# Two narrow key tiles of a diagonal in one attention step, and the transposes of a block ahead of both copies

## The chip, the cores and the metric

The kernel runs on one core of a Trainium2 chip, in 32-bit floats throughout. The metric is the device time of one launch in microseconds (us), the median of several runs; lower is better. The core has five engines that work beside each other and wait for each other through semaphores: TensorE (PE in the profile, PEld for its weight loads), VectorE (DVE), ScalarE (ACT), GpSimd (POOL) and SyncE (SP), which here issues most of the DMAs. Each takes its own instructions in order.

## The reference, as far as it matters

The input x is 4096 tokens (32 nodes by 128 time steps) of 256 features. Layer 0 is a pre-normed attention over all 4096 tokens with 8 heads of 32, and a residual; a query of time t sees all keys of time up to t, at every node:

```
x  = (h - mu) / sqrt(var + eps) * ln_g + ln_b
q  = x @ wq.T + bq + sym_emb            # then Q, K, V through in_w; K and V from h, not normed
scores = einsum('bqhd,bkhd->bhqk', Q, K) / sqrt(32)
t = tile(arange(128), 32);  scores = where(t[None, :] > t[:, None], -inf, scores)
ctx = softmax(scores) @ V
h  = h + alpha * (ctx @ out_w.T + out_b)
```

Layer 1 is a banded attention of width 24 and a mixture of 8 experts with two hidden layers each. The change does not touch layer 1.

## The kernel before

**Tiling.** The tokens are sorted by time, so that the mask is block-triangular: 8 blocks of 512 queries (`BLK`, `NBLK`), keys in tiles of 128 (4 time steps by 32 nodes, `P`). Block b attends to key tiles 0 to 4b+3. The first 4b+1 of them are of use to all 512 queries; the last three of the four on the diagonal are of use to the last 384, 256 and 128 queries alone. These three are the narrow tiles. The 8 heads lie in two groups of 4 (`NGRP`, `HG`), a group's 4 heads of 32 features on the 128 partitions.

**A step** is one key tile of one group of one block: 8 x 2 x 4(b+1), 288 steps in all. In it

- `scores` (L1273) makes 4 matmuls, one head each, on 4 row tiles of the array: head 0 into the bank `sa` (pool `ps_a`, one buffer), heads 1 to 3 into three banks `sb` (pool `ps_b`, two buffers). Every matmul of 32-bit floats shows as two passes in the trace;
- `exps` (L1288) makes two exponentials on ScalarE, one of `sa`, one of `sb`, into an SBUF tile `pt` (pool `pp`, 5 buffers); on a diagonal tile POOL then zeroes what the mask forbids inside the 128 x 128 corner, in three memsets (L1298);
- `add` (L1301) adds `pt` to the running sum `acc` on DVE, two heads to an instruction (L1314), which gives the softmax's denominators;
- `product` (L1318) makes 4 matmuls with the values, one head each, on 4 column tiles, into the one bank `av` that stays open for a group's whole pass.

**The order of the work.** It is written out by hand in the loop at L1451 (`manual_schedule`: each engine takes its instructions in the order of the program). Iteration n issues scores of step n, the product of step n-2 (`LAG`), the exponentials of n with a group's last copy of `av` (`evacuate`, L1338) between the two, the add of step n-1, and then what else is due. `key_order` (L1251) spreads the three narrow tiles evenly among the full ones, so each is a step of its own.

**What else is due.** `todo` is the preparation of the next block in pieces (`prep`, L1033): the transposition of its inputs (`transposed_x`, L979: for each of two halves of the features four transposes into a bank, then a ScalarE copy), two projections for keys, two for values, two for queries. They are spread evenly over the steps of the block (L1499), each takes a `ps_b` buffer. Two iterations after a group's last scores its last product is made; one later `close_sums` (L1345) sums `acc` over the partitions with a matrix of ones; in blocks 6 and 7 the last one and two tiles (`direct`, L1267) are not added on DVE but summed there by TensorE too. Six iterations after the last product comes `invert` (reciprocal, and two DMAs on SP that spread it, L1391 and L1394), twelve after it `scale` (DVE, L1402). `stat_at` (L1433) gives the iterations at which DVE takes the layer norm's statistics of blocks 2 to 7, two tiles an iteration from n = 0 to 11; when the last is taken, `rstd_block` (L952) has ScalarE take a square root, for which it changes its function table and back. `load_at` (L1437) gives the iterations at which SP issues the loads for them. In the last group of block 7 POOL adds a bias to 12 tiles of tokens (L1523, L904), from its fifth step on.

Of the kernel before, what the change touches and what calls it, by code (L numbers as in the profile page):

```python
# [10 lines left out]
F32 = mybir.dt.float32  # L11
# [5 lines left out]
P = 128  # L17
# [806 lines left out]
def fast_kernel(ctx: ExitStack, tc: tile.TileContext, ins: dict, out: bass.AP, narrow):  # L824
# [101 lines left out]
    with ExitStack() as l0:  # L926
# [52 lines left out]
        def transposed_x(b, pss):  # L979
            xg = xblk[b]  # L980
            hT = px.tile([P, 2, BLK], F32, tag="hT", name=f"hT{b}", bufs=1)
            for c in range(2):
                for i in range(TPB):
                    nc.tensor.transpose(
                        pss[c][:, i * P : (i + 1) * P], xg[:, i, c * P : (c + 1) * P], ident
                    )
                nc.scalar.copy(hT[:, c, :], pss[c])
            return hT
# [249 lines left out]
        with ExitStack() as at:  # L1238
# [12 lines left out]
            def key_order(b):  # L1251

                n = TPB * (b + 1)
                order, part = list(range(n - TPB + 1)), list(range(n - 1, n - TPB, -1))
                if b == 0:
                    return list(range(n))
                for i, j in enumerate(part):
                    order.insert((i + 1) * n // TPB, j)
                return order

            orders = [key_order(b) for b in range(NBLK)]
            steps = [
                (b, g, j)
                for b in range(NBLK) for g in range(NGRP) for j in orders[b]
            ]

            direct = [orders[b][TPB * (b + 1) - max(0, b - NBLK + 3) :] for b in range(NBLK)]  # L1267

            LAG = 2
            first_col = lambda b, j: max(0, j - TPB * b) * P  # L1270
            raw, held, live, open_av = {}, {}, {}, {}

            def scores(b, g, j):  # L1273
                q = qblk[b]
                lo = first_col(b, j)
                sa = ps_a.tile([P, BLK], F32, tag="a", name=f"sa{b}_{g}_{j}")
                sb = ps_b.tile([P, HG - 1, BLK], F32, tag="b", name=f"sb{b}_{g}_{j}")
                for h in range(HG):
                    rows = slice(h * HD, (h + 1) * HD)
                    nc.tensor.matmul(  # L1280
                        (sb[:, h - 1, :] if h else sa)[:, lo:],
                        lhsT=kT[rows, g, j * P : (j + 1) * P],
                        rhs=q[rows, g, lo:],
                        start=True, stop=True,
                    )
                raw[b, g, j] = sa, sb

            def exps(b, g, j, between):  # L1288
                lo = first_col(b, j)
                pt = pp.tile([P, HG, BLK], F32, tag="pt", name=f"pt{b}_{g}_{j}")  # L1290
                sa, sb = raw.pop((b, g, j))
                nc.scalar.activation(pt[:, 0, lo:], sa[:, lo:], AF.Exp, scale=SCALE)  # L1292
                between()
                nc.scalar.activation(pt[:, 1:, lo:], sb[:, :, lo:], AF.Exp, scale=SCALE)  # L1294
                if j >= TPB * b:

                    for k in range(1, TT):
                        nc.gpsimd.memset(pt[k * N : (k + 1) * N, :, lo : lo + k * N], 0.0)  # L1298
                held[b, g, j] = pt

            def add(b, g, j):  # L1301

                if j == orders[b][0] or j in direct[b]:
                    return
                pt, lo = held[b, g, j], first_col(b, j)
                if j == orders[b][1]:
                    old = held[b, g, orders[b][0]]
                    live[b, g] = ap.tile([P, HG, BLK], F32, tag="acc", name=f"acc{b}_{g}")
                    if lo:
                        nc.vector.tensor_copy(live[b, g][:, :, :lo], old[:, :, :lo])  # L1310
                else:
                    old = live[b, g]
                for hs in (slice(0, HG // 2), slice(HG // 2, HG)):
                    nc.vector.tensor_tensor(  # L1314
                        live[b, g][:, hs, lo:], old[:, hs, lo:], pt[:, hs, lo:], op=ALU.add
                    )

            def product(b, g, j):  # L1318
                if j == orders[b][0]:
                    open_av[b, g] = ps_av.tile([P, BLK], F32, tag="av", name=f"av{b}_{g}")  # L1320
                av = open_av[b, g]
                pt, lo = held[b, g, j], first_col(b, j)
                for h in range(HG):
                    nc.tensor.matmul(  # L1324
                        av[h * HD : (h + 1) * HD, lo:],
                        lhsT=v[:, j, (g * HG + h) * HD : (g * HG + h + 1) * HD],
                        rhs=pt[:, h, lo:],
                        start=(j == orders[b][0]), stop=(j == orders[b][-1]),
                    )
# [15 lines left out]
            def close_sums(b, g):  # L1345

                sums = banks(f"sums{b}_{g}", 1)[0]
                parts = [held.pop((b, g, j)) for j in direct[b]] + [live.pop((b, g))]
                for k, part in enumerate(parts):
                    for h in range(HG):  # L1350
                        nc.tensor.matmul(  # L1351
                            sums[h * HD : (h + 1) * HD, :], lhsT=ones, rhs=part[:, h, :],
                            start=(k == 0), stop=(k == len(parts) - 1),
                        )
# [69 lines left out]
            def begin_projections():  # L1424
# [8 lines left out]
            stat_at = {  # L1433
                2 * (b - 2) + k: [(b, 2 * k), (b, 2 * k + 1)]
                for b in range(2, NBLK) for k in range(2)
            }
            load_at = {3: ("xs", 5, 6), 4: ("xs", 7), 6: ("xg", 2), 8: ("xg", 3)}  # L1437
# [13 lines left out]
            for n in range(len(steps) + LAG + 1 + 16):  # L1451
                if n < len(steps):
                    b, g, j = steps[n]
                    own = NGRP * TPB * (b + 1)
                    k = orders[b].index(j)
# [16 lines left out]
                    scores(b, g, j)  # L1472
                ends = None
                if 0 <= n - LAG < len(steps):
                    if n - LAG == len(steps) - 1:
                        begin_projections()
                    product(*steps[n - LAG])
                    bb, gg, jj = steps[n - LAG]
                    if jj == orders[bb][-1]:
                        ends = bb, gg  # L1480
                        later.setdefault(n + 1, []).append((close_sums, ends))
                        if ends != LASTU:
                            later.setdefault(n + 6, []).append((invert, ends))
                            later.setdefault(n + 12, []).append((scale, ends))

                def between():
                    if ends:
                        evacuate(*ends)

                if n < len(steps):  # L1490
                    exps(b, g, j, between)
                else:
                    between()
                if 0 <= n - 1 < len(steps):
                    add(*steps[n - 1])
                if n < len(steps):
                    at_step = g * TPB * (b + 1) + k + 1
# [992 lines left out]
```

## Time and profile before

| what | value |
|---|---|
| median of 3 runs | 1527.48 us (1526.95 to 1528.06) |
| the profiled execution, its own time | 1528.81 us |
| its span | 1526.8 us |
| mean granted TensorE clock | 0.997 |
| layer 0's steps, first scores to the last add | 19.1 to 733.3 us |
| from there to the end | 793.5 us |
| ScalarE, an exponential of 128x512 / 128x1536 | 598 / 1451 ns |
| DVE, an add of 128x1024 | 1217 ns |

By block of layer 0, from its first scores to the next block's (us, of the profiled execution):

| block | from | length | PE busy | DVE busy | ScalarE busy |
|---|---|---|---|---|---|
| 0 | 19.11 | 32.67 | 31.76 | 17.21 | 17.22 |
| 1 | 51.78 | 46.72 | 43.35 | 33.96 | 34.88 |
| 2 | 98.50 | 69.17 | 65.14 | 53.62 | 47.14 |
| 3 | 167.67 | 79.63 | 77.95 | 65.86 | 62.13 |
| 4 | 247.30 | 99.00 | 96.52 | 87.35 | 78.79 |
| 5 | 346.30 | 113.31 | 111.20 | 103.77 | 93.36 |
| 6 | 459.61 | 130.04 | 127.94 | 119.04 | 108.89 |
| 7, to the last add | 589.65 | 143.62 | 139.78 | 136.64 | 123.02 |

Reading it: busy time counts an engine's instructions without overlap; a matmul's end is modelled, so a PE that is busy all the time need not run at its peak. What an engine waited for stands in brackets behind an instruction of the timeline: the idle time ahead of it, and the instruction that ended it. "pt L1294" is the exponential of three heads, "pt L1292" that of the first.

### The profile page before, as it was taken

To read this page: it belongs to the slowest core of one execution; us is meant where nothing else is said; L and a number is where in the kernel's file an instruction comes from. 1 tells how busy PE (TensorE), PEld (TensorE's weight loads), DVE (VectorE), ACT (ScalarE), POOL (GpSimd) and SP (SyncE) were. 2 spreads that over 40 slices of the span, in tenths; PEclk is the share of its full clock that TensorE was granted. 3 is DMA by queue.
4 is the path that set the end of the run, shared out by engine and by line. 5 is a ranking of instruction groups with operands and counts; after the bars stand their busy time and mean duration, and the time that the engine had idled before them with its cause. 6 is when DMAs were issued, how large, how long until landed. Compare 5 with 4: busy or idle time off the path is not lost.

```text
span 1526.8 us, 23826 instructions
## 1 busy us (share of the span) xinstructions
PE 1477.1 (97%) x8873; PEld 836.9 (55%) x8873; DVE 1200.6 (79%) x2193; ACT 940.8 (62%) x1402; POOL 163.9 (11%) x387
## 2 busy tenths in 40 slices
PE   8999999999999999999999999999999999999998
PEld 5333232232222222222557887888888788788887
DVE  5667879898899898999746777777786777677775
ACT  4667777877888888988445444544355454544443
POOL 2110003000000000031062002100010000000000
PEclk9999999999999999999999999999999999999999
DMA  6111101010000010000332343333433334343442
GB/s 140 35 43 26 29 8 31 9 29 8 1 15 9 1 49 15 8 9 1 116 116 92 102 132 109 121 104 112 129 121 120 106 104 138 103 128 111 138 152 64
DMA packets 96378, 110.16 MB, mean 72 GB/s; under 512 B 17949, under 2 KB 85232, under 8 KB 96256
## 3 DMA queue, kind: packets, MB, share of 16 engines
q1 hardware_dynamic: 93280, 106.87, 23.5%
q8 instruction: 72, 1.18, 0.3%
q0 software_dynamic: 1888, 0.91, 0.3%
q10 hardware_dynamic: 1088, 0.79, 0.2%
q14 instruction: 50, 0.41, 0.1%
HBM read 98.87 MB, written 8.53 MB: 70 GB/s over the span
## 4 chain that ended last, share of the span: by engine, by line
PE 75%; DVE 12%; ACT 7%; issue 4%; DMA 0%; POOL 0%; ACTq 0%; DVEq 0%; POOLq 0%
PE psh L1948 18%; PE sa L1280 15%; PE av L1324 14%; PE psy L2005 11%; DVE acc L1314 2%; ACT h L1931 2%; PE psv L1026 2%; PE psq L1005 2%; PE psk L992 2%; ACT pt L1294 2%; PE psk L1697 2%; PE sb L1280 1%; PE sums L1351 1%; DVE h L1990 1%; ACT pt L1292 1%
## 5 line engine op out<-in xcount | busy, mean ns | idle before, releaser
L1314 DVE TENSOR_TENSOR acc<-acc,pt 128x1024 f32<-128x1024 f32 (+3 forms) x500 | 529.3, 1127 | 40.7 <-ACT pt L1294 28.4
L1294 ACT ACTIVATE pt<-sb 128x1536 f32<-128x1536 f32 (+3 forms) x288 | 387.6, 1346 | 3.2 <-PE sb L1280 3.0
L1280 PE MATMUL sa<-q,kT 32*128 32x512 f32 (+3 forms) x576 | 303.1, 606 | 9.4 <-ACT pt L1292 7.1
L1280 PE MATMUL sb<-q,kT 32*128 32x512 f32 (+3 forms) x1728 | 307.0, 606 | 1.8 <-ACT pt L1294 0.7
L1931 ACT ACTIVATE h<-h,bshift,bscale 128x256 f32<-128x256 f32 x244 | 159.1, 699 | 221.5 <-DVE h L1990 221.5
L1324 PE MATMUL av<-pt,v 128*32 128x512 f32 (+3 forms) x2304 | 287.1, 571 | 1.5 <-ACT big_t L1339 0.4
L2005 PE MATMUL psy<-wo,h 128*128 128x256 f32 x1024 | 242.8, 380 | 0.0
L1292 ACT ACTIVATE pt<-sa 128x512 f32<-128x512 f32 (+3 forms) x288 | 162.2, 563 | 95.6 <-PE sb L1280 63.9
L2005 PEld LDWEIGHTS psy<-wo,h 128*128 128x128 f32 x1024 | 192.0, 190 | 28.9 <-issue 2.9
L1280 PEld LDWEIGHTS sa<-q,kT 32*128 32x128 f32 x576 | 84.5, 183 | 220.6 <-ACT pt L1292 179.4
L1324 PEld LDWEIGHTS av<-pt,v 128*32 128x32 f32 x2304 | 45.6, 108 | 200.4 <-issue 183.2
L2013 DVE SCALAR_TENSOR_TENSOR tokens<-psy,w,tokens 128x256 f32<-128x256 f32 x256 | 111.0, 475 | 34.9 <-PE psy L2005 34.6
L1975 DVE TENSOR_TENSOR u<-psh,u 128x256 f32<-128x256 f32 x122 | 51.0, 418 | 104.1 <-ACT u L1974 103.8
L1298 POOL MEMSET pt<- 32x128 f32 (+2 forms) x192 | 58.5, 304 | 627.0 <-ACT pt L1294 523.5
L1931 ACT ACTIVATE h<-psh,bshift,bscale 128x256 f32<-128x256 f32 (+1 forms) x132 | 75.6, 574 | 45.8 <-PE psh L1948 38.7
L1280 PEld LDWEIGHTS sb<-q,kT 32*128 32x128 f32 x1728 | 88.3, 183 | 9.1 <-ACT pt L1294 5.8
L1974 ACT COPY u<-psh 128x256 f32<-128x256 f32 x122 | 43.9, 360 | 79.6 <-PE psh L1948 79.2
L1948 PE MATMUL psh<-tx,s 128*128 128x256 f32 x366 | 90.3, 383 | 0.3 <-DVE tx L1921 0.3
L1948 PE MATMUL psh<-th,s 128*128 128x256 f32 x366 | 89.0, 379 | 0.0
L1990 DVE TENSOR_TENSOR h<-psh,u 128x512 f32<-128x512 f32 x122 | 83.1, 681 | 4.2 <-PE psh L1948 4.2
L1948 PEld LDWEIGHTS psh<-tx,s 128*128 128x128 f32 x366 | 70.1, 192 | 10.3 <-DVE tx L1921 0.7
L1948 PE MATMUL psh<-xfT,w 128*128 128x256 f32 x244 | 74.0, 385 | 1.1 <-DVE u L1975 1.1
(332 smaller groups left out, 1764.5 us busy)
## 6 DMA issues: line engine op xcount, KB each, us to landing
w<-in_L_ffn_W_dram SPq DMA_DIRECT2D x128, 256.0 KB
s<-kept SPq DMA_DIRECT2D x56, 512.0 KB
wo<-in_L_ffn_Wo_dram SPq DMA_DIRECT2D x64, 256.0 KB
xg<-in_x_dram SPq DMA_DIRECT2D x32, 128.0 KB
tokens<-in_x_dram SPq DMA_DIRECT2D x8, 512.0 KB
kept<-s SPq DMA_DIRECT2D x8, 512.0 KB
out_dram<-tokens SPq DMA_DIRECT2D x32, 128.0 KB
rec<-flat SPq DMA_DIRECT2D x60, 64.0 KB
```

The lines of the kernel that those rows point to most:

```text
L1280: nc.tensor.matmul((sb[:, h - 1, :] if h else sa)[:, lo:], lhsT=kT[rows, g, j * P : (j + 1) * P], rhs=q[rows, g, lo:], start=True, stop=True,)
L1292: nc.scalar.activation(pt[:, 0, lo:], sa[:, lo:], AF.Exp, scale=SCALE)
L1294: nc.scalar.activation(pt[:, 1:, lo:], sb[:, :, lo:], AF.Exp, scale=SCALE)
L1298: nc.gpsimd.memset(pt[k * N : (k + 1) * N, :, lo : lo + k * N], 0.0)
L1314: nc.vector.tensor_tensor(live[b, g][:, hs, lo:], old[:, hs, lo:], pt[:, hs, lo:], op=ALU.add)
L1324: nc.tensor.matmul(av[h * HD : (h + 1) * HD, lo:], lhsT=v[:, j, (g * HG + h) * HD : (g * HG + h + 1) * HD], rhs=pt[:, h, lo:], start=(j == ...
L1931: nc.scalar.activation(dst, src, AF.Relu, bias=bshift[:, m, k : k + 1], scale=bscale[:, m, k : k + 1])
L1948: nc.tensor.matmul(ps, lhsT=w, rhs=x, start=start, stop=True, skip_group_check=True)
L1975: nc.vector.tensor_tensor(u, a[:, 1], u, op=ALU.add)
L1990: nc.vector.tensor_tensor(flat.rearrange("p (k c) -> p k c", k=2), self.q, self.u.unsqueeze(1).to_broadcast([P, 2, HB]), op=ALU.add,)
L2005: nc.tensor.matmul(ps[:, i, :], lhsT=ht[:, c, r * P : (r + 1) * P], rhs=wo[k][:, c, :], start=(c == 0), stop=(c == 1),)
L2013: nc.vector.scalar_tensor_tensor(out=tokens(n), in0=ps[:, i, :], scalar=w[:, r, e : e + 1], in1=tokens(n), op0=ALU.mult, op1=ALU.add,)
```

## The change

1. `transposed_x` makes all eight transposes of a block first and then the two copies; before, the second four stood behind the first copy.
2. A group's pass is now a list of steps of parts (`unit_steps`). A part is (group, key tile, first query, place in the bank, width). The tiles of 384 and of 128 queries make one step (`both`): the 128 go to columns 0 to 127, the 384 to columns 128 to 511 of the same banks. From block 1 on, group 0's last step holds its own tile of 256 queries and the same tile of group 1 side by side; group 1 uses it from there (`carried`): its product comes with that of group 1's first step, its add with group 1's first add. In block 0 the 256 stay a step of their own.
3. So there are 265 steps instead of 288: 6 in block 0, 8b+5 in block b. A merged step has 8 matmuls of scores, two exponentials, three memsets and one `pt`. The preparation's pieces are spread over the fewer steps.
4. The adds: 384 in two instructions, 128 in one of four heads; the carried 256 in two, and group 1's first pair of tiles then in four of 256 columns. `direct` keeps one tile of each group in block 6 and two in block 7; of group 0 in block 7 these are the last full tile and its half of the shared step, in block 6 the last full tile.
5. The statistics take ten iterations, three tiles in each of the first four, and the loads for them move up by one iteration.

```diff
@@ transposed_x
                         pss[c][:, i * P : (i + 1) * P], xg[:, i, c * P : (c + 1) * P], ident
                     )
+            for c in range(2):
                 nc.scalar.copy(hT[:, c, :], pss[c])
@@ the steps
-            orders = [key_order(b) for b in range(NBLK)]
-            direct = [orders[b][TPB * (b + 1) - max(0, b - NBLK + 3) :] for b in range(NBLK)]
+            def unit_steps(b, g):
+                n = TPB * b
+                order = [[(g, j, 0, 0, BLK)] for j in range(n + 1)]
+                both = [(g, n + 1, P, P, BLK - P), (g, n + 3, BLK - P, 0, P)]
+                order.insert((n + 2) // 2, both)
+                if not b:
+                    order.append([(g, n + 2, BLK // 2, 0, BLK // 2)])
+                elif not g:
+                    order.append(
+                        [(k, n + 2, BLK // 2, k * BLK // 2, BLK // 2) for k in range(NGRP)]
+                    )
+                return order
+            for b, count in ((NBLK - 2, 1), (NBLK - 1, 2)):
+                last = len(units[b, 0]) - 1
+                direct[b, 0] = tuple(range(last - 1, last - 1 + count))
+                last = len(units[b, 1]) - 1
+                direct[b, 1] = tuple(range(last + 1 - count, last + 1))
@@ scores
-                for h in range(HG):
-                    nc.tensor.matmul(
-                        (sb[:, h - 1, :] if h else sa)[:, lo:],
-                        lhsT=kT[rows, g, j * P : (j + 1) * P],
-                        rhs=q[rows, g, lo:],
+                for gg, j, lo, at, w in units[b, g][k]:
+                    for h in range(HG):
+                        nc.tensor.matmul(
+                            (sb[:, h - 1, :] if h else sa)[:, at : at + w],
+                            lhsT=kT[rows, gg, j * P : (j + 1) * P],
+                            rhs=q[rows, gg, lo : lo + w],
@@ add
+                if k == 0 and more:
+                    for hs in HEADS:
+                        nc.vector.tensor_tensor(
+                            live[b, g][:, hs, lo:], pt[:, hs, lo:], other[:, hs, at : at + w],
+                            op=ALU.add,
+                        )
...
+                    if more:
+                        z = more[1][2]
+                        for hs in HEADS:
+                            nc.vector.tensor_tensor(
+                                live[b, g][:, hs, :z], first[:, hs, :z], pt[:, hs, :z],
+                                op=ALU.add,
+                            )
+                            nc.vector.tensor_tensor(
+                                live[b, g][:, hs, z:], live[b, g][:, hs, z:], pt[:, hs, z:],
+                                op=ALU.add,
+                            )
+                        return
...
+                for _, _, lo, at, w in parts:
+                    for hs in HEADS if w > P else (slice(0, HG),):
@@ product
+                todo = [(held[b, g, k], p) for p in units[b, g][k] if p[0] == g]
+                if not k and carried(b, g):
+                    todo.append(carried(b, g))
+                for i, (pt, (_, j, lo, at, w)) in enumerate(todo):
+                    for h in range(HG):
+                        nc.tensor.matmul(
+                            av[h * HD : (h + 1) * HD, lo : lo + w],
@@ statistics and loads
-            stat_at = {
-                2 * (b - 2) + k: [(b, 2 * k), (b, 2 * k + 1)]
-                for b in range(2, NBLK) for k in range(2)
-            }
-            load_at = {3: ("xs", 5, 6), 4: ("xs", 7), 6: ("xg", 2), 8: ("xg", 3)}
+            for n in range(10):
+                count = 3 if n < 4 else 2
+                stat_at[n], tiles_left = tiles_left[:count], tiles_left[count:]
+            load_at = {2: ("xs", 5, 6), 3: ("xs", 7), 5: ("xg", 2), 7: ("xg", 3)}
@@ the loop
-                    own = NGRP * TPB * (b + 1)
+                    own = sum(len(units[b, i]) for i in range(NGRP))
```

## The prediction

> **What bounds the kernel now.** I read the page first, then the stretches of layer 0 block by block, then the timeline of a narrow tile, of a transposition and of a change of head group.
>
> ```profile
> PE 1477.1 (97%) x8873; PEld 836.9 (55%) x8873; DVE 1200.6 (79%) x2193; ACT 940.8 (62%) x1402; POOL 163.9 (11%) x387
> ...
> PE 75%; DVE 12%; ACT 7%; issue 4%; DMA 0%; POOL 0%; ACTq 0%; DVEq 0%; POOLq 0%
> ```
>
> TensorE holds three quarters of the chain, but a share over the whole span hides stages. Of the stretches (start:end, its length, then busy time of PE, PEld, DVE, ACT, POOL), these are block 6 and the last 64 us of layer 0:
>
> ```profile
> 459.61:589.65 130.04, 127.94 (x961) 33.97 (x961) 119.04 (x114) 108.89 (x122) 7.35 (x25) 1.00 0.06 18
> ...
> 669.49:733.27 63.78, 60.96 (x488) 15.48 (x484) 63.77 (x56) 53.48 (x58) 15.44 (x23) 1.00 0.03 9
> ```
>
> In block 6 PE is full and DVE has 11 us to spare; in the last head group of block 7 DVE is full. So an edit pays in blocks 0 to 6 what it takes from PE, and in block 7 what it takes from DVE's adds. A narrow tile on PE, in block 6 (start, length, instruction):
>
> ```profile
> 541.48 1.06 PE L1324 MATMUL av<-pt,v 128*32 128x512 f32 x8
> 542.48 0.37 PE L1280 MATMUL sa<-q,kT 32*128 32x128 f32 x1
> ...
> 542.69 0.27 PE L1280 MATMUL sa<-q,kT 32*128 32x128 f32 x1
> ...
> 542.91 1.07 PE L1324 MATMUL av<-pt,v 128*32 128x512 f32 x8
> ...
> 545.97 0.69 PE L1280 MATMUL sa<-q,kT 32*128 32x512 f32 x1
> ...
> 547.04 0.43 PE L1324 MATMUL av<-pt,v 128*32 128x128 f32 x8
> 547.78 0.69 PE L1280 MATMUL sa<-q,kT 32*128 32x512 f32 x1 [0.31 <-ACT pt L1292]
> ```
>
> Each matmul is two passes. Scores of 512 columns take 1.07 us (545.97 to 547.04), a product of 512 1.00, together the 2.07 us a full step takes. Scores of 128 take 0.43 (542.48 to 542.91), and their product 0.74 (547.04 to 547.78): 0.31 of it is PE waiting until ScalarE has read the one sa bank. A small product cannot cover that exponential.
>
> **The transposes** (all of one block's eight before either copy). Today PE stops between the halves:
>
> ```profile
> 108.19 0.65 PE L984 MATMUL pst<-ident,xg 128*128 128x128 f32 x4
> 108.88 0.59 ACT L987 COPY hT<-pst 128x512 f32<-128x512 f32 x1 [1.07 <-PE pst L984]
> ...
> 109.52 0.66 PE L984 MATMUL pst<-ident,xg 128*128 128x128 f32 x4 [0.68 <-ACT hT L987]
> ```
>
> The second four need nothing of that copy but its place in the order. Seven blocks (1 to 7) are transposed inside the step loop; PE's gaps there are 0.68 us six times and 0.95 once (at 61.45): 5.0 us. The copies then lie back to back on ScalarE while PE runs the next scores, 1.07 us, and ScalarE had waited 1.07 us for the first. I take the whole 5.0; the least, if exponentials are then late, is 2.
>
> **384 with 128.** By the same reading at 573.66 and 578.69, a 384 tile costs 0.89 for scores and 0.78 for its product, 1.67; the 128 costs 0.43 + 0.74 = 1.17. Removed: 2.84. Added is one step of 512 columns, but in twice the matmuls. The mean score pass in the groups by shape is 642, 533, 426 and 321 ns for 512, 384, 256 and 128 columns, so 107 ns per 128; passes start 0.53 and 0.21 apart for 512 and 128, so about 0.1 of each pass is paid whatever its width. The merged scores have four passes, 1.07 + 0.21 = 1.28, which agrees with 0.89 + 0.43 = 1.32; I take 1.30. Products fall 607, 498, 391, 285, the same slope; 1.00 less 2 x 0.43 leaves 0.14 per set, so merged products take 1.14. Step: 2.44; gain 0.40. It is now long enough that nobody waits for the sa bank. The bounds: 2.07, if the second set's fixed part hides (gain 0.77), and no gain.
>
> [...] The second set goes to the same four row groups. A weight load takes 183 ns in the scores and 108 in the products (rows of PEld); exposed for each of the two added passes this is 0.37 + 0.22 = 0.59 on top, 3.03 for the pair, a loss of 0.19. But the row at 542.69 is a second pass to the same row groups, 0.21 after the first and not 0.107 + 0.183 = 0.29. I go by the row.
>
> **256 with the other group's 256.** Today both cost 0.65 (492.14 to 492.79) + 0.74 (498.83 to 499.57) = 1.39, 2.78 a block. The shared step stands last in group 0; its scores take 1.30 beside a full product of 1.00. Its own product falls on the change of group, where ScalarE waits for the last product to copy it out:
>
> ```profile
> 464.20 1.04 ACT L1339 COPY big_t<-av 128x512 f32<-128x512 f32 x1 [0.76 <-PE av L1324]
> ```
>
> That product is now 256 wide, 0.57 instead of 1.00, and the copy 0.43 earlier. The carried product, 0.57, comes one step later, just before the sums, where PE waits for ScalarE anyway (0.21, then 0.8 between the sa and sb scores at 467.57 and 468.39). Best: 1.30 + 1.00 - 0.43 = 1.87, gain 0.91; with the carried product bare, 2.44, gain 0.34. ScalarE's wait is in the rows, so nearer the best: 0.70.
>
> **ScalarE** loses 46 of its exponentials (two for each of 23 steps): at 128 columns one takes 291 ns against 598 for 512, so about 0.19 is fixed, 8.7 us in all. PE's full step is 2.07 and ScalarE's about 1.95, so beyond the waits counted this saves nothing.
>
> **Blocks.** Blocks 1 to 6: 2 x 0.40 + 0.70 = 1.50 each, 9.0. Block 0 has 384 with 128 twice and no carried tile; projections lie between its products, so there is no sa wait to remove, and the sums are equal: 0.
>
> **Statistics and loads** of the start come in ten steps instead of twelve, up to three a step; 0.6 us each on DVE, which is busy 17.2 of block 0's 32.7 us. The loads move up one step on SP's queue; their buffers come free in the same order, and block 5's statistics stand two steps behind its load. Nothing. But the square root of the deviations, with its two table loads (63.70 to 66.51), now follows a step with one projection, whose kT copy (0.69) stands before it on ScalarE, and the step after it has no projection for PE, where one of 1.98 ran at 63.99. Behind it on ScalarE wait the next exponentials, and PE for their bank. From the merged scores (0): product done 2.3, projection 4.2, copy 4.95, tables 7.75, exponential 8.35; PE's next scores and product end at 6.3. It waits 2.05 where it waited 0.99: 1.1 lost (bounds 0 and 2). On SP, rb's wait of about 8 us (L976) now stands ahead of block 1's flat and rec in block 2; rec has six steps and some projections, about 16 us, and comes about when scale wants it. DVE behind it has slack there: nothing, at most 1.
>
> **Block 7, DVE.** A full add pair takes 2.27 us (two at 1.135) against PE's 2.07, so DVE falls behind from 602.21 on: 131.1 us to the end at 733.27, of which 2.0 idle between the groups. By the new order group 0 adds one full tile more (+2.27) and not the 256 (-1.21); the 128 goes in one instruction (0.60 for 0.67, twice). Group 1 adds the carried 256 (1.21) in place of its own, and splits its first pair in four (2.42 for 2.27). Work: +1.1. The idle 2.0 closes, for the carried add can start a step earlier. POOL's bias additions (L904) stretch an add from 1217 to about 1750 ns, 0.535 more start to start, nine times now; no memset stands between the first eleven any more, and they fall on a full DVE: about 12 times, +1.6, less where they overlap nothing as the first ones today (I take +0.7). Block 7: 2.0 - 1.1 - 0.7 = 0.2 gained (bounds -1.5 and +1.5). What PE gains there is lost to this.
>
> **Sum.** 5.0 + 9.0 + 0 - 1.1 + 0.2 = 13.1 of the profiled execution's 1528.8, of which 1526.8 is span: 1515.7. That execution is 1.3 above the median 1527.48, so the forecast is 1514.3. Layer 1 keeps its instructions and starts as much earlier.
>
> **The rivals.**
> - *The second set is free*: each pair costs 2.07. Twelve pairs gain 0.37 more: 1509.9. For it: records of the four heads overlap within 20 ns. Against it: the passes' fixed part is paid already between passes. 0.14.
> - *DVE becomes the bound earlier*, from block 5 on. Blocks 5 and 6 then lose 2 x (1.5 + 0.68) = 4.4: 1518.7. For it: 119.0 of 130.0 busy in block 6. Against it: PE's gain there is 2.2 and DVE's slack 11. Pairs that gain little end here too. 0.17.
> - *Same row groups*: [...] 0.05.
> - *Slower*: all eight weight loads of an added set are exposed one by one, 8 x 183 + 8 x 108 ns = 2.33 us, 2.0 over the 0.35 counted. On 18 steps that is 36 lost, 1537. It decides from 0.73 us a step (13.1 / 18). The 0.43 scores at 542.48 contain eight loads and speak against it. 0.03.
> - The forecast: 0.61.
>
> It can't fail to do what it says: the order of PE's queue shows the eight transposes together and the merged steps.
>
> **Range.** From free second sets with block 7's better end, 1508.5, to small pairs and a dearer start, 1520.5. A measurement can tell about 0.2% (3 us) from no change. Faster by more: 0.61 + 0.14 + 0.17 = 0.92; within: 0.05; slower: 0.03.
>
> **What would show it.** The gap at pst gone, seven times. Merged scores 1.3 us and their products 1.14, step about 2.44. The copy of av at a change from group 0 to 1 0.4 earlier behind the product. PE's wait near the table load about 2 us. DVE without idle from block 7's third step to the last sums, and POOL's twelve additions early in it. If DVE is idle at block 7's end, or PE waits for pt buffers in block 5 or 6, I am wrong.

## The result, and the profile after

The changed kernel takes 1516.92 us (median of 4 runs, 1515.38 to 1517.62), beside 1527.77 for the kernel before on the same chip (4 runs, 1526.95 to 1529.86): a ratio of 0.9926, 95% interval 0.9908 to 0.9943, a gain of 10.9 us. The profiled execution took 1517.62, its span 1515.8 (before: 1528.81 and 1526.8). The forecast was 1514.3.

The page of the changed kernel, busy time of each engine and the chain of waits by engine:

```profile
PE 1472.3 (97%) x8873; PEld 843.4 (56%) x8873; DVE 1205.0 (79%) x2191; ACT 941.3 (62%) x1356; POOL 166.6 (11%) x318
...
PE 70%; DVE 17%; ACT 6%; issue 5%; DMA 0%; POOL 0%; ACTq 0%; DVEq 0%; POOLq 0%
```

PE's matmuls are as many as before, 8873; ScalarE has 46 fewer instructions. The chain moved from PE (75%) to DVE (12% to 17%): more of the kernel is now bound where this change gives nothing. The stretches of the changed kernel show where (start:end, length, then PE, PEld, DVE, ACT, POOL, the granted clock): block 5, block 6, the last 64 us of layer 0, and layer 1 with what leads to it.

```profile
333.77:448.60 114.83, 113.16 (x826) 31.35 (x825) 106.84 (x103) 93.77 (x100) 6.43 (x16) 0.99 0.04 8
448.60:575.86 127.26, 126.86 (x961) 34.55 (x961) 118.32 (x114) 109.31 (x116) 6.49 (x16) 1.00 0.06 18
656.00:719.80 63.80, 59.70 (x468) 15.02 (x460) 63.66 (x53) 52.55 (x54) 20.76 (x20) 1.00 0.04 9
719.80:1515.80 796.00, 769.69 (x3687) 626.95 (x3685) 574.25 (x1509) 367.32 (x731) 74.57 (x151) 0.99 0.36 116
```

Block 6 took 130.04 before and gained 2.8. Block 5 took 113.31 before and is 1.5 *longer*. The end of layer 0 is DVE's as before, with more of POOL's work beside it (20.76 where it was 15.44). Layer 0's last add ends at 719.80 instead of 733.27, 13.5 earlier, close to the forecast sum of 13.1. But layer 1, the same instructions, takes 796.0 where it took 793.5, and gives back 2.5.

The merged step of block 6, on PE in the changed kernel:

```profile
476.74 0.69 PE L1299 MATMUL sa<-q,kT 32*128 32x512 f32 x1
...
477.81 1.07 PE L1389 MATMUL av<-pt,v 128*32 128x512 f32 x8
478.80 0.58 PE L1299 MATMUL sa<-q,kT 32*128 32x384 f32 x1
...
479.23 0.48 PE L1299 MATMUL sa<-q,kT 32*128 32x384 f32 x1
...
479.55 0.27 PE L1299 MATMUL sa<-q,kT 32*128 32x128 f32 x1
...
479.66 0.27 PE L1299 MATMUL sa<-q,kT 32*128 32x128 f32 x1
...
479.88 1.06 PE L1389 MATMUL av<-pt,v 128*32 128x512 f32 x8
480.88 0.69 PE L1299 MATMUL sa<-q,kT 32*128 32x512 f32 x1
```

A full step's scores run from 476.74 to 477.81, 1.07 us. The merged scores, four passes, run from 478.80 to 479.88: 1.08, not the 1.30 of the forecast. The next step starts 2.08 after it (480.88). The passes themselves start 0.43, 0.32, 0.11 and 0.22 apart: 0.107 for each 128 columns, and about 0.21 more in all. The products of the merged tile take 1.01 (sixteen passes, 484.01 to 485.02), those of a full one 1.00; every merged step of blocks 2 to 6 that stands between steps without a projection is 2.07 or 2.08 long.

The transposes of block 5, on PE, without their gap:

```profile
351.09 1.07 PE L1389 MATMUL av<-pt,v 128*32 128x512 f32 x8
352.09 1.09 PE L984 MATMUL pst<-ident,xg 128*128 128x128 f32 x8
353.11 0.69 PE L1299 MATMUL sa<-q,kT 32*128 32x512 f32 x1
```

From 352.09 to the next scores are 1.02. Before, the same eight ran from 362.50 to 364.42, 1.92: the gain is 0.90, not the 0.68 of the gap alone.

What block 5 lost, on PE near its end:

```profile
432.83 1.12 PE L1299 MATMUL sa<-q,kT 32*128 32x512 f32 x2
434.74 1.13 PE L1299 MATMUL sb<-q,kT 32*128 32x512 f32 x6 [0.79 <-DVE q L1010]
435.81 1.94 PE L1389 MATMUL av<-pt,v 128*32 128x512 f32 x8
437.67 1.21 PE L1299 MATMUL sa<-q,kT 32*128 32x512 f32 x1
...
438.69 0.86 PE L1299 MATMUL sa<-q,kT 32*128 32x512 f32 x1
```

and on DVE at the same place:

```profile
429.48 4.61 DVE L1375 TENSOR_TENSOR acc<-acc,pt 128x1024 f32<-128x1024 f32 x4
434.02 0.67 DVE L1010 TENSOR_TENSOR q<-psq,rb 128x512 f32<-128x512 f32 x1
```

The projection of the queries was done by 430.8. Its bank is one of the two that the sb scores use, and DVE empties it (L1010) in the order of its queue, behind four adds: 434.02. So PE has the sa scores done and waits 0.79 for an sb bank. Then comes something else: the product takes 1.94 where it takes 1.06, and score passes start 1.02 apart for 0.53. The granted clock there is 0.50:

```profile
434.00:436.00 2.00, 1.26 (x10) 0.50 (x14) 1.97 (x4) 0.65 (x2) 0.00 (x0) 0.95 0.00 0
436.00:437.00 1.00, 1.00 (x8) 0.01 (x2) 1.00 (x2) 1.00 (x1) 0.00 (x0) 0.50 0.00 0
```

The clock's records show it at one half for 3.41 us from 435.82, which costs a busy PE half of it, 1.7 us. The same kind of wait stands at 337.4 (0.47 us, for q), and in block 2 at 155.2 (1.57, for woT). In the kernel before, the sb scores never waited for q, and 0.68 us for woT.

Two later runs have the same work in block 5 and no half clock there. One of them (the run with the old statistics), block 5 and the same wait:

```profile
340.57:453.80 113.23, 111.57 (x826) 31.12 (x825) 105.22 (x102) 93.81 (x100) 6.45 (x16) 1.00 0.04 8
```

```profile
439.65 1.12 PE L1299 MATMUL sa<-q,kT 32*128 32x512 f32 x2
441.56 1.13 PE L1299 MATMUL sb<-q,kT 32*128 32x512 f32 x6 [0.79 <-DVE q L1010]
442.62 1.06 PE L1389 MATMUL av<-pt,v 128*32 128x512 f32 x8
443.62 0.69 PE L1299 MATMUL sa<-q,kT 32*128 32x512 f32 x1
```

So without the half clock block 5 takes 113.2, as long as before (113.3). The 1.5 is the clock, and the waits take back what the change gains in this block. The wait also costs more than its 0.79. The sb passes, which otherwise run beside the sa passes, now run behind them, and this step takes 3.97 us (439.65 to 443.62) instead of 2.07.

### The profile page after: what moved, and what is told of

It is laid out like the page before. It is cut to its first block, busy times and chain, and to the rows that moved or that the text cites. A ratio compares the mean times of both kernels' runs of the same rounds, so it can differ in the third digit from the quotient of the medians.

```text
span 1515.8 us, 23636 instructions
## 1 busy us (share of the span) xinstructions
PE 1472.3 (97%) x8873; PEld 843.4 (56%) x8873; DVE 1205.0 (79%) x2191; ACT 941.3 (62%) x1356; POOL 166.6 (11%) x318
## 4 chain that ended last, share of the span: by engine, by line
PE 70%; DVE 17%; ACT 6%; issue 5%; DMA 0%; POOL 0%; ACTq 0%; DVEq 0%; POOLq 0%
PE psh L2017 18%; PE sa L1299 13%; PE av L1389 12%; PE psy L2074 11%; DVE acc L1375 6%; ACT h L2000 3%; PE psk L993 2%; PE psv L1027 2%; PE psq L1006 2%; PE sb L1299 2%; PE psk L1766 2%; DVE h L2059 1%; PE sums L1419 1%; ACT pt L1314 1%; DVE tokens L2082 1%
## 5 line engine op out<-in xcount | busy, mean ns | idle before, releaser
L1375 DVE TENSOR_TENSOR acc<-acc,pt 128x1024 f32<-128x1024 f32 (+2 forms) x470 | 523.8, 1178 | 35.7 <-POOL pt L1326 20.9
L1314 ACT ACTIVATE pt<-sb 128x1536 f32<-128x1536 f32 (+1 forms) x265 | 382.8, 1445 | 6.2 <-PE sb L1299 6.1
L1299 PE MATMUL sa<-q,kT 32*128 32x512 f32 (+3 forms) x576 | 297.5, 602 | 8.7 <-ACT pt L1312 5.4
L1299 PE MATMUL sb<-q,kT 32*128 32x512 f32 (+3 forms) x1728 | 301.2, 603 | 3.2 <-DVE woT L1059 1.6
L1389 PE MATMUL av<-pt,v 128*32 128x512 f32 (+3 forms) x2304 | 283.1, 571 | 0.5
L1312 ACT ACTIVATE pt<-sa 128x512 f32<-128x512 f32 (+1 forms) x265 | 157.9, 596 | 80.5 <-PE sb L1299 44.2
L1326 POOL MEMSET pt<- 32x256 f32 (+4 forms) x123 | 52.1, 424 | 609.3 <-ACT pt L1314 521.9
L2000 ACT ACTIVATE h<-psh,bshift,bscale 128x256 f32<-128x256 f32 (+1 forms) x132 | 75.6, 574 | 46.7 <-PE psh L2017 39.1
L2017 PEld LDWEIGHTS psh<-th,s 128*128 128x128 f32 x366 | 70.3, 192 | 9.9 <-DVE h L2059 0.2
## 6 DMA issues: line engine op xcount, KB each, us to landing
xg<-in_x_dram SPq DMA_DIRECT2D x32, 128.0 KB
out_dram<-tokens SPq DMA_DIRECT2D x32, 128.0 KB
```

The costliest lines, as they stand in the source:

```text
L1299: nc.tensor.matmul((sb[:, h - 1, :] if h else sa)[:, at : at + w], lhsT=kT[rows, gg, j * P : (j + 1) * P], rhs=q[rows, gg, lo : lo + w], s ...
L1312: nc.scalar.activation(pt[:, 0, used], sa[:, used], AF.Exp, scale=SCALE)
L1314: nc.scalar.activation(pt[:, 1:, used], sb[:, :, used], AF.Exp, scale=SCALE)
L1326: nc.gpsimd.memset(rows, 0.0)
L1375: nc.vector.tensor_tensor(acc[:, hs, cols], acc[:, hs, cols], pt[:, hs, at : at + w], op=ALU.add,)
L1389: nc.tensor.matmul(av[h * HD : (h + 1) * HD, lo : lo + w], lhsT=v[:, j, (g * HG + h) * HD : (g * HG + h + 1) * HD], rhs=pt[:, h, at : at + w],
```

## The experiments

**The transposes alone**, put into the kernel before:

```diff
             for c in range(2):
                 for i in range(TPB):
                     ...
+            for c in range(2):
                 nc.scalar.copy(hT[:, c, :], pss[c])
```

> The kernel before, with only the eight transposes put ahead of the two copies. Theory: the seven gaps at pst (six of 0.68 us and one of 0.95) are gone and nothing comes late behind the two copies: 5.0 us less than before, about 1522.7. Rival: the two copies back to back (1.07 us) make the next exponentials late and give part of it back: 2 us less, about 1525.7.

Measured: 1522.14, ratio 0.9958 (0.9944 to 0.9971), 6.4 us. Its trace gains 0.68 to 1.2 in each of blocks 0 to 6, 6.6 in layer 0, and the copies cost nothing: in block 5 they run from 358.51 to 359.58, and PE's steps go on 2.06 apart (358.40, 360.46). By time this is the first theory (the interval is 4.4 to 8.6 us); the trace shows a little more than its 5.0, because block 5, for one, gains 0.22 beside the 0.68 of its gap: the eight take 1.02 (357.38 to 358.40), where the two fours took 0.66 and 0.58.

**Without the shared tile**, from the changed kernel:

```diff
-                if not b:
-                    order.append([(g, n + 2, BLK // 2, 0, BLK // 2)])
-                elif not g:
-                    order.append(
-                        [(k, n + 2, BLK // 2, k * BLK // 2, BLK // 2) for k in range(NGRP)]
-                    )
+                order.append([(g, n + 2, BLK // 2, 0, BLK // 2)])
...
-                direct[b, 1] = tuple(range(last + 1 - count, last + 1))
+                direct[b, 1] = tuple(range(last - 1, last - 1 + count))
...
-                if b and g:
+                if False:
```

> The changed kernel without the shared tile: each head group has its own 256 step again, for scores, adds and product; the 384 with 128 steps and the transposes stay. Theory (a merged step costs 2.07 us, as the trace of the changed kernel shows): blocks 1 to 6 lose per block what the shared tile brings, 2.78 less 2.07 or a little more (the copy at the change of group comes 0.43 earlier): 0.7 to 1.1 each, 4 to 7 us over the changed kernel's 1516.9, so 1521 to 1524. Rival (the shared tile brings only the 0.34 of its worst case, because its carried product lies bare at the change of group): 2 us more, 1519. In both, the merged 384 with 128 step stays at 2.07 us.

Measured: 1525.57, ratio 0.9983 (0.9975 to 0.9991), 8.7 us over the changed kernel. More than either theory, and not clean: PE's sb scores wait for banks that DVE empties, 1.80 us at 159.5 (woT), 2.33 at 250.0 (bnT), 0.90 at 348.2 and 0.97 at 446.9 (the query product), and three half-clock stretches, one of them of double length, fall into its layer 0 (mean granted clock of this execution 0.995, before 0.997). So the wait of block 5 is not the shared tile's doing; what the tile is worth is taken up again in the last run.

**The two sets of one head directly after each other** in the scores:

```diff
-                for gg, j, lo, at, w in units[b, g][k]:
-                    for h in range(HG):
+                for h in range(HG):
+                    for gg, j, lo, at, w in units[b, g][k]:
```

> The changed kernel with the merged steps' score matmuls in the order of the heads: the two sets of one head directly after each other, on the same row group, where in the changed kernel the four heads of one set come first. Theory A (what the changed kernel shows holds for any order: no weight load is exposed): the merged step stays at 2.07 us, and the time at 1516.9 within 1 us. Theory B [...]: in each merged step four loads of 184 ns come bare, up to 0.74 us, or once for each of the two float32 passes, 1.5 us; the scores of a merged step then last 1.8 to 2.5 us where they last 1.07, and 20 merged steps of blocks 0 to 6 cost 10 to 30 us: 1527 to 1547.

Measured: 1516.5, ratio 0.9917 (0.9903 to 0.9930): no change. Theory A holds. The merged scores of block 6 in this kernel's trace:

```profile
480.13 0.59 PE L1299 MATMUL sa<-q,kT 32*128 32x384 f32 x1
...
480.99 0.27 PE L1299 MATMUL sa<-q,kT 32*128 32x128 f32 x1
...
481.23 1.06 PE L1389 MATMUL av<-pt,v 128*32 128x512 f32 x8
```

1.10 us (480.13 to 481.23), 0.02 more than in the changed kernel, with the second set's loads ordered directly behind matmuls on the same row group.

**The query product ahead of the add** on DVE, from the changed kernel:

```diff
-                if 0 <= n - 1 < len(steps):
-                    add(*steps[n - 1])
                 if n < len(steps):
                     ...
                     while done < count * at_step // own and not (closing and b):
                         next(todo, None)
                         done += 1
+                if 0 <= n - 1 < len(steps):
+                    add(*steps[n - 1])
```

> The changed kernel with the add of a step issued behind the step's projection, not ahead of it: VectorE multiplies the projected queries (the line of q<-psq,rb) one add pair, 2.27 us, earlier in its order. Theory (in block 5 of the changed kernel VectorE lags, holds the psq bank about 5 us, and TensorE waits 0.47 and 0.79 us at 337 and 434 for the next sb bank; the second wait is followed by 3.4 us at a granted clock of 0.50): both waits go, and with them the 1.7 us at the low clock: block 5 takes 112.2 us or less instead of 114.8, and the time falls by 2 to 4 us to 1513 to 1515. Rival (the waits belong to something else that is late, and the low clock comes anyway): block 5 stays at 114.8 and the time at 1516.9.

Measured: 1510.3, ratio 0.9879 (0.9864 to 0.9894), which is 0.47% or 7 us less than the changed kernel, more than expected. DVE in block 5 of this run, the same query product:

```profile
427.17 2.34 DVE L1375 TENSOR_TENSOR acc<-acc,pt 128x1024 f32<-128x1024 f32 x2
429.44 0.68 DVE L1010 TENSOR_TENSOR q<-psq,rb 128x512 f32<-128x512 f32 x1
```

The edit moves all of a step's preparation on DVE ahead of the add, the copies of woT and bnT too. The query product now follows one add pair and is done before the sb bank is asked for; PE's steps there are 2.07 throughout. Block 5 takes 110.1 instead of 114.8; block 2 gains 1.2 (the wait for woT is 0.34), block 4 1.0, block 6 0.7 and block 7 0.9, while block 3 loses 0.8. Of block 5's 4.7, the step with the wait at 434 is 1.9, the clock window 1.6, and the first four steps, with the wait at 337, 1.2. Block 3's loss is a wait of 0.71 for the load of the expert norms, which PE now reaches sooner.

**The statistics and loads as before**, in the changed kernel:

```diff
-            for n in range(10):
-                count = 3 if n < 4 else 2
-                ...
-            load_at = {2: ("xs", 5, 6), 3: ("xs", 7), 5: ("xg", 2), 7: ("xg", 3)}
+            stat_at = {
+                2 * (b - 2) + k: [(b, 2 * k), (b, 2 * k + 1)]
+                for b in range(2, NBLK) for k in range(2)
+            }
+            load_at = {3: ("xs", 5, 6), 4: ("xs", 7), 6: ("xg", 2), 8: ("xg", 3)}
```

> The changed kernel with the statistics and loads of the start placed as before: two statistics a step, twelve steps, the square root two steps later. Theory (the prediction's term): TensorE's wait at the table loads, 2.15 us in the changed kernel at 65.63, goes back to about 1.0, and block 1 takes 1.1 us less than its 45.4; the time falls by 1.1, which the runs can hardly tell. Rival: the square root then stands behind another projection's copy in the shorter order of steps, so the wait is 2 us or more at its new place: no gain.

Measured: 1523.23, ratio 0.9971 (0.9960 to 0.9981): nearly 7 us *slower* than the changed kernel. Neither theory had this, which shows in the timeline of PE in block 1:

```profile
58.26 1.16 PE L984 MATMUL pst<-ident,xg 128*128 128x128 f32 x8 [4.34 <-DMA xg<-in_x_dram]
```

Block 0 has two steps fewer now. At its old step number the load of block 2's tokens stands at the head of block 1, and the transposes wait 4.34 us for it. Together with half-clock windows at 59.1 and 79.6 block 1 is 6.3 us longer. The wait at the table loads did not go back to 1.0 either; it is 2.34 at its new place (78.3). So the earlier loads, which the forecast counted as nothing, spare block 1 that wait.

**Without the bias additions of block 7**, from the run with the query product ahead:

```diff
-                    if b == NBLK - 1 and g and 4 <= k < 4 + FIRST:
-                        with_bias(k - 4)
```

> The kernel of the run e4_q_first without GpSimd's twelve bias additions of block 7 (the bias of the first twelve tiles of tokens is left out). Theory (in block 7 VectorE's queue of adds sets the end, and each of the twelve additions stretches an add from 1.135 to about 1.67 us start to start): VectorE's work in block 7 falls by 12 x 0.535 = 6.4; TensorE stands idle 5.3 us there, so the end comes 4 to 5.3 us earlier, and the time at about 1505.5. Rival (the stretch is paid only while VectorE is ahead, or the scale and sums set the end): less than 1.5 us, 1509 to 1510.

Measured: 1503.68, ratio 0.9844 (0.9831 to 0.9857). Block 7 falls from 143.1 to 137.4 us: the twelve additions cost 5.7, nearly the whole 6.4 of stretched adds. In the run with the query product ahead six adds take 6.89 at 634.87, 1.15 each, and the eight from 648.29, beside POOL's additions, 13.43, 1.68 each.

**The bias additions in block 6**:

```diff
+            token_at = {(NBLK - 2, 0, i): i for i in range(3)}
+            token_at[NBLK - 1, 0, 0] = 3
...
-                    if b == NBLK - 1 and g and 4 <= k < 4 + FIRST:
-                        with_bias(k - 4)
+                    if b == NBLK - 2 and 6 <= k < 6 + FIRST // 2:
+                        with_bias(g * FIRST // 2 + k - 6)
```

> The kernel of the run e4_q_first with the twelve bias additions in block 6, six in each head group from its seventh step on, and the first three loads of tokens at the head of block 6, where VectorE has 9 us to spare. Theory (VectorE sets the end of block 7, not of block 6): block 7 falls by 4 to 5.3 us as without the additions, block 6 stays within 0.5 us of its 126.6; time about 1505.5. Rival (six stretched adds in a row make VectorE late by 3.2 us, more than its buffers hold, and the wait moves to block 6): block 6 2 to 4 us longer, and the time at 1508 to 1510.

Measured: 1504.65, ratio 0.9856 (0.9840 to 0.9873). Block 7 is 137.5, as without them, but block 6 is 130.4 for 126.6. POOL took the six right behind its last zeroing of block 5, not at the seventh step, and PE's sums at the change of block waited for the stretched adds (POOL's timeline, then PE's):

```profile
441.80 0.99 POOL L1326 MEMSET pt<- 32x128 f32 x3 [20.96 <-ACT pt L1314]
442.87 8.79 POOL L904 TENSOR_TENSOR tokens<-tokens,outb 128x256 f32<-128x256 f32 x6
...
451.22 3.50 PE L1419 MATMUL sums<-acc,ones 128*32 128x512 f32 x8 [1.96 <-DVE acc L1375]
```

The sums then ran at half clock (3.50 for eight, where the changed kernel's take 1.06 at 455.24; a window from 451.7). SP had issued the loads of the tokens at 414.4 to 426.7, well ahead, so it was POOL's queue that the additions followed; the expectation of the next run has this otherwise.

**The same, tied to the middle of the group**, behind the merged tile's zeroing on POOL's queue:

```diff
-                    if b == NBLK - 2 and 6 <= k < 6 + FIRST // 2:
-                        with_bias(g * FIRST // 2 + k - 6)
+                    if b == NBLK - 2 and 14 <= k < 14 + FIRST // 2:
+                        with_bias(g * FIRST // 2 + k - 14)
```

> The kernel of the run e7_bias_early with the six bias additions of each head group of block 6 issued from its fifteenth step on, behind the merged tile's zeroing on GpSimd's queue. In the run e7_bias_early GpSimd took them at once when the tokens had landed (442.87 to 451.66), at the change of block, where the sums wait for the last add (TensorE idle 1.96 us). Theory (only that place was dear, and mid-group VectorE's slack takes the stretch): block 6 at 126.6 to 127.2 us where it was 130.4, block 7 stays at 137.5: 2 to 3.5 us less than that run, 1501.5 to 1503. Rival (six stretched adds make VectorE late wherever they stand, and the lag lasts to the next change of group): block 6 at 128 or more, time 1504 or more.

Measured: 1504.99, ratio 0.9842 (0.9826 to 0.9859). Block 6 is 128.3 (63.3 in its first group as without additions, 64.9 in its second, which keeps 1.6 of the lag), block 7 138.3. The two runs can't be told apart by time. Block 6 and the time are what the rival named (128 or more, 1504 or more); only the first group went as the theory had it. Against the changed kernel they are faster by 0.7% and 0.85% (0.9856 and 0.9842 over 0.9926): the fastest complete kernels of the study.

**Four tiles summed by TensorE at the end**, from the run with the query product ahead:

```diff
+            last = len(units[NBLK - 1, 1])
+            direct[NBLK - 1, 1] = tuple(range(last - 4, last))
```

> The kernel of the run e4_q_first with the last four tiles of the last head group summed by TensorE, not the last two. Theory (VectorE sets the end of block 7): two add pairs less, 2 x 2.27 = 4.5 us, and two more sets of sums on TensorE, 2 x 1.0 us, which lie partly behind the last exponentials: the end comes 2 to 4 us earlier, time 1506.5 to 1508.5. Rival (TensorE is as full as VectorE by then, and the sums stand bare at the end): no gain or 2 us lost, 1510 to 1512.

Measured: 1509.65, ratio 0.9879 (0.9863 to 0.9894): no change, the rival. DVE in this run, at its last add:

```profile
702.86 6.89 DVE L1377 TENSOR_TENSOR acc<-acc,pt 128x1024 f32<-128x1024 f32 x6
716.23 0.66 DVE L1436 RECIPROCAL rec_last<-sums 128x80 f32<-128x80 f32 x1 [6.48 <-PE sums L1421]
```

DVE ends its adds at 709.75, and waits 6.48 for the sums, which PE can begin only at 711.68, after its own last products. With two tiles this wait is 1.16.

**Without the shared tile, query product ahead**: the edit of the second run on the fourth.

> The kernel of the run e4_q_first without the shared tile, each head group with its own 256 step (as in e2_pairs_only). Theory (the waits for VectorE's query product, 0.9 to 2.3 us at four places of e2_pairs_only, hid what the parts are worth): those waits go, a block of pairs alone takes 1.5 us less (2 x 0.77) than the same block with the transposes alone, and what is left against e4_q_first is the shared tile: the forecast's 0.70 a block gives 4 us (1514.5), the best of its bounds, 0.91 and the merged step at 2.07, up to 1.1 a block gives 6.5 us (1517). Rival (the shared tile's worth is the 1.4 a block that e2_pairs_only shows against the changed kernel): 8.5 us, 1519.

Measured: 1515.94, ratio 0.9918 (0.9903 to 0.9933), 5.6 to 6 us over the kernel with the shared tile: inside the theory's 4 to 6.5, under the rival's 8.5. By blocks (us, from a block's first scores to the next one's; block 7 to its last add):

| block | 0 | 1 | 2 | 3 | 4 | 5 | 6 | 7 |
|---|---|---|---|---|---|---|---|---|
| before | 32.7 | 46.7 | 69.2 | 79.6 | 99.0 | 113.3 | 130.0 | 143.6 |
| transposes alone | 31.8 | 46.0 | 68.0 | 78.5 | 98.1 | 112.4 | 129.2 | 143.6 |
| and pairs, query product ahead | 31.3 | 46.6 | 67.0 | 76.8 | 97.2 | 111.3 | 128.0 | 144.3 |
| and shared tile, query product ahead | 31.3 | 45.4 | 65.3 | 77.3 | 94.2 | 110.1 | 126.6 | 143.1 |
| changed kernel | 31.3 | 45.4 | 66.5 | 76.5 | 95.2 | 114.8 | 127.3 | 143.9 |

The clean blocks of this run (block 4 holds a half-clock window and a wait of 1.78 for bnT, which also has to come behind the adds, block 2 waits of 0.64 and 1.85 for woT and bvb) give pairs 1.1 to 1.6 a block (blocks 3, 5, 6; block 1 loses 0.6, with the longer wait at the table load) and the shared tile 1.2 to 1.4 (blocks 1, 5, 6). Block 7 of this run holds a half-clock window too (687.8). The layer's 9.3 between the two kernels is more than the time shows, because the profiled run with the shared tile has two such windows in layer 1 and this one none. Block 3 goes the other way by 0.5: with the shared tile it comes to the transposition of the expert norms before their load (bn) is in, and PE waits 0.71 at 238.2.

Where the shared tile's gain comes from shows in block 6. Group 0's own 256 step, in this run, and then the shared step of the run with it:

```profile
510.48 0.48 PE L1293 MATMUL sa<-q,kT 32*128 32x256 f32 x1
...
512.12 0.69 PE L1293 MATMUL sa<-q,kT 32*128 32x512 f32 x1
```

```profile
503.98 0.48 PE L1299 MATMUL sa<-q,kT 32*128 32x256 f32 x1
...
506.05 0.69 PE L1299 MATMUL sa<-q,kT 32*128 32x512 f32 x1
```

The own step takes 1.64, the shared one 2.07, 0.43 more; but group 1's own step, another 1.64, is gone. That is 1.21 gained. The carried product is nearly free: the step in which it falls, with the sums, takes 4.22 us where it takes 4.18 without it.

## Why the prediction was right, and by which steps

The time lies in the range and the likeliest case came near, but by errors of opposite sign: the nearness is luck. Layer 0 gained 13.3 between its first scores and its last add; the table splits it as 6.6 (transposes) + 5.0 (pairs) + 9.3 (shared tile) - 7.6 (query product behind the adds). Of the middle two the sum, 14.3, is firmer than the split, because of the half-clock windows in blocks 4 and 7 of the run between them; and what the query order alone does in the kernel before was not tried (nothing waits for q there). The last term holds every block's difference between the changed kernel and the one with the query product ahead, one clock window of 1.7 among it.

- *Transposes, 5.0*: right in mechanism, undersized: 6.6. The step "PE's gaps there are 0.68" left out 0.22 for each stop: the four before the gap take 0.66 to their end and the four behind it 0.58 to the next scores, 1.24 together, where eight in a row take 1.02 (and 1.92 less 1.02 is 0.90).
- *384 with 128, gain 0.40*: the failed term is "about 0.1 of each pass is paid whatever its width". Two narrow rows of two passes each can't tell a cost per pass from a cost per set; I read the first. The merged rows show the second: beside 0.107 for each 128 columns of a pass, about 0.21 for one step's scores, with four passes (1.08) as with two (1.07 and 0.43). So the bound 2.07 was the right value, the rival with the second set free: 0.77 a pair by PE's rows, 0.6 to 0.8 by the clean blocks.
- *Shared tile, 0.70*: 1.2 to 1.4 in clean blocks, above my best bound of 0.91. With the scores at 1.07 instead of 1.30 that bound would have been 1.14. The comparison is not quite the forecast's: in the run without the shared tile the own 256 steps stand last as well, so the earlier copy of av, as forecast by 0.43 (3.84 us after group 1's first scores, 4.27 before), is in both. What is left shows in the steps of block 6, above: 1.21. What standing last costs the own steps was not tried alone.
- *Same row groups* (0.05): this rival is the estimate of 0.59 a step for weight loads of 183 and 108 ns that lie bare; on 18 merged steps it would have taken back 10.6, to 1524.9. The merged step at 2.07, and the order by heads at 1.10 for the scores, show nothing of it in these float32 matmuls. Weighing the row at 542.69 (0.21 from pass to pass, not 0.29) over it was right.
- *Statistics, loads, table load*: PE waits 2.15 at the table load (2.05 forecast). "Nothing" for the loads is right for the net, but it hid that the old places would have cost 4.34.
- *Block 7, +0.2*: it lost 0.3. That POOL's additions fall on a full DVE was right; the run without them prices all twelve at 5.7.
- *What was missed*: the sb bank held behind DVE's adds. The second rival had DVE bite from block 5 on, through the adds and pt buffers. It did bite there, but through the queries' bank, with DVE only one or two add pairs late and idle 8 us in the block. It comes with the pairs: the transposes alone wait for no q, and the waits are 0.90 and 0.97 without the shared tile, 0.47 and 0.79 with it. Putting the preparation ahead of the add is worth 7 us by time, so this cost is shown; 1.7 of it is the clock window of block 5 in the profiled run.
- *"Layer 1 starts as much earlier"*: it ends 2.5 less early. Two half-clock windows fall into its 796.0, one into the 793.5 before. In the other runs that part takes 791.7 to 792.4 with none, 793.9 to 794.2 with one and 795.6 to 795.8 with two (the run with four tiles summed by TensorE aside). So each window is worth about 1.8 there; the other 0.7 of the 2.5 was not traced.
- *"Slower"*: the sum of this rival is wrong. 36 us more than the forecast's 1514.3 is 1550, not 1537. It did not come.

## What to carry to other kernels

Before costing merged narrow matmuls, find out if the fixed part of a short group is paid per matmul or per group (here 0.21 for one step's scores, with two passes or four); rows of two passes can't tell. When an engine in a shared pipeline gets shorter steps, look at each bank that a lagging engine must empty (PE waited 0.47 and 0.79 for the queries' bank in block 5), and issue that small eviction ahead of its long queue work. Loads and side work pinned to step numbers must be placed anew when the steps get fewer, and side work on a free queue need not run at the step where it is written: POOL took the additions written at the seventh step of block 6 at 442.87, 0.08 behind its last zeroing of block 5.

## What the hardware showed beside this

TensorE's granted clock fell to 0.50 for 3.41 us at a time: twice in the profiled execution of the kernel before (from 162.19 and 793.65) and four times in the changed kernel's (from 155.92, 435.82, 780.56 and 1060.46), the last microseconds aside. The places differ in kernels whose code is the same there. The changed kernel and the run without bias additions have the same work at the table load of block 1 and the same wait for it. The changed kernel, then the other (stretches, the clock in the third column from the end):

```profile
68.00:70.00 2.00, 2.00 (x25) 0.71 (x18) 1.71 (x3) 2.00 (x3) 0.00 (x0) 1.00 0.00 0
```

```profile
68.00:70.00 2.00, 2.00 (x12) 0.51 (x16) 1.68 (x4) 1.71 (x2) 0.00 (x0) 0.64 0.00 0
```

The clock in these 2 us was 1.00 in the one and 0.64 in the other. PE waited 2.15 us in the one and 2.16 in the other just before; only the second lost 1.6 us in block 1 (47.0 for 45.4). So a wait of this length was followed by half clock in one execution and not in the other. In the 10 us ahead of the changed kernel's four stretches PE's longest waits were 1.57, 0.79, 0.59 and 1.44, all shorter than the 2.15 that none followed. What decides where the clock falls these runs do not show.

For a comparison of single traces it means that 1.7 us come and go with each stretch.
